# The last tile of a down product on row halves of the array, next to the attention scores, and new durations in a list schedule

## The chip, the cores and the metric

The kernel runs on one core of a Trainium2 chip. The core has five engines with a queue of instructions each: TensorE (PE in the profile, with its weight loads as PEld), VectorE (DVE), ScalarE (ACT), GpSimd (POOL) and SyncE (SP, which issues the DMAs). They wait for each other through semaphores. The metric is the time of one execution on the device in microseconds (us).

## The reference

Everything is float32. The input x is 2 batches of 4096 tokens with 256 channels. Two blocks follow each other, each added to its input.

```python
# first block: a recurrence over the tokens, 256 channels side by side
x = x + group_norm(sigmoid(r) * wkv(k, v)) @ W_o.T       # r, k, v: products of mixed tokens
# second block: DEPTH = 2 layers of this
h = shift_token(x)                        # half of the channels come from the token before
q, k, v = split(h @ wqkv)                 # 8 heads of 64
q, k = rotary_xpos(l2norm(q) * qs, l2norm(k) * ksc)
sim = q @ k.T ; attn = softmax(sim)       # blocks of 128 tokens, own block and the one before
x = x + (attn @ v) @ wo
h = layernorm(shift_token(x)) * lg + lb
a, g = split(h @ w1 + b1)                 # 682 columns each
x = x + (a * gelu(g)) @ w2 + b2
```

The hidden width is 682 = 5 x 128 + 42. Together with a row of ones, which carries the bias b2, the last line is a product over 683 rows: five tiles of 128 rows and one of 43.

## The kernel before, in words

**Tiling.** A window is 128 tokens, a block of tokens four windows (512 tokens). The two layers over two batches give 32 blocks and 128 windows, numbered n = 0 to 127. Window n has its attention at its own place in the program; the feed-forward part (the hidden product with `w1`, the gelu, the product with `w2`, called the down product) is done per block, one block later, in portions (`fill`) put between the attention parts of the windows that follow. The recurrence of batch 0 is done ahead of window 0; that of batch 1 is cut into 16 chunks of 256 tokens (`rec2`), and chunk c is put at window `int(c * R_SLOTS / rec2.n)`: windows 0, 3, 6, 10 and so on to 50.

**One window's attention.** Four score banks are written by eight pairs of matmuls over 64 rows (`scores`): the even head of a pair works on the rows 0 to 63 of the array and the odd head on the rows 64 to 127. In the same unbroken run of TensorE instructions (a `piece`) stands `values(n - 1)`, the product of the probabilities of the window before with its v, on column halves of the array. `softmax` then works on one score bank after the other: a masked copy, a minimum, two exponentials with their sums, a reciprocal, and two scalings (`scaled`). `transpose_p` first adds one column of the probabilities to the next (on VectorE, four heads at once), and transposes the probabilities on TensorE.

**The feed-forward part of block k.** `gate` makes five hidden tiles of 128 rows and copies them to `hm`; `remainders` makes the 42 rows that are left of both halves; `gelus` runs over the six tiles of `hm`; `value` multiplies the other half in; `down(k, w)` multiplies the six tiles of `hm` with `w2` for window w of the block, six matmuls of 128 rows by 256 columns into one bank, adds the bank to x, and sends x out. The sixth tile is filled up with rows that meet zeros of `w2`, and takes a matmul over 128 rows as the others do. In the profile each float32 matmul of the program stands as two instructions.

**What sets the order.** The program notes all operations with a row number (`plan.at`), and a list scheduler (`Plan.order`) then decides the order on every engine: it keeps a clock for each engine, takes the operation that can start first, and among those that can start within 1 ns of each other the one with the lowest row. It works with durations that are written down in `Plan.cost` and `TURN` (what it charges TensorE for a change between the full array, row halves and column halves), and with eight PSUM banks: a piece that opens several banks is placed only when so many are free. An operation noted on `either` goes to ScalarE or VectorE, to whichever can begin it first. The order that comes out is fixed in the program; on the chip each queue just follows it and waits where it must.

Nearly all instructions are issued by one line (L503), so the profile's groups are told apart by tiles: `bank<-w,hm` is the down product, `bank<-kT,qT` the scores, `bank<-pT,vt` and `bank<-pB,dv` the values, `bank<-wqkv,xT` the q, k and v products, `bank<-hT,w` the hidden products, `bank<-wo,oT` the attention's output product, `bank<-mats,...` transposes. L497 and L499 are the scalings on VectorE and ScalarE.

Of the kernel before, what the change touches and what calls it, by code (L numbers as in the profile page):

```python
# [15 lines left out]
P = 128  # L16
# [17 lines left out]
R_SLOTS = 54  # L34
# [24 lines left out]
TURN = {"row": 195, "col": 95, "full": 95}  # L59
# [114 lines left out]
class Plan:  # L174
# [119 lines left out]
    def cost(self, o):  # L294
# [19 lines left out]
        elif o.eng == "vector":  # L314
            if name == "tensor_tensor_reduce":
                d = 210 + 1.05 * n
            elif name == "tensor_tensor_scan":
                d, o.lock = 2.48 * n, True
            elif name in ("scalar_tensor_tensor", "tensor_tensor"):
                d, o.lock = 175 + 1.04 * n, wide > 1  # L320
            elif name in ("tensor_scalar", "tensor_copy") and not psum:
                d, o.lock = 230 + 0.45 * n, n > 64
            elif name == "bn_aggr":
                d = 180
            elif name == "reciprocal":
                d = 165 + 4 * n
            else:
                d = 150 + 1.04 * n
            o.step, o.time = max(d - 70, 60), d
        elif o.eng in ("scalar", "either"):  # L330
            d = 160 + 0.83 * n
            if name == "scaled":
                d = 40 + 1.4 * n
            if name == "activation":
                o.set = SETS.get(o.args[2])
                if "accum_out" in o.kw:
                    d += 320
                elif o.args[2] in (AF.Gelu, AF.Identity):
                    d = 40 + 1.4 * n
            o.step, o.time = d - 100, d  # L340
        elif o.eng == "gpsimd":
            if name == "tensor_tensor":
                d = 600 + 160 * n if ALU.pow in o.args else 150 + 2.25 * n
                o.lock = n > 64
            elif name == "tensor_scalar":
                d = 200 + 1.12 * n
                o.lock = n > 64
            else:
                d = 170 + 0.98 * n
                o.lock = n > 64  # L350
# [10 lines left out]
    def order(self):  # L361
# [47 lines left out]
        while todo:  # L409
# [23 lines left out]
            for o in g:  # L433
# [12 lines left out]
                if o.eng == "either" and e == "vector":  # L446
                    n = o.outs[0].idx.size
                    time = 150 + 1.04 * n if o.name == "copy" else 230 + 0.45 * n
                    step = time - 70
                    o.lock = o.name == "scaled"  # L450
# [56 lines left out]
def kernel(ctx: ExitStack, tc: tile.TileContext, a: dict, out: bass.AP):  # L507
# [322 lines left out]
    def weights(l, which):  # L830
# [6 lines left out]
        if "1" in which:  # L837
            nc.sync.dma_start(out=w1, in_=a["w_1"][l])
            nc.sync.dma_start(out=w2, in_=a["w_2"][l])
# [5 lines left out]
    hm = tile_of([P, NM, T], "hm")  # L845
# [6 lines left out]
    xs, xTs, hs, x1s, zs, hTs, rems = ({} for _ in range(7))  # L852
# [179 lines left out]
    def scores(n):  # L1032
# [8 lines left out]
        with piece():  # L1041
            if n:
                values(n - 1)
            for hp in range(HEADS // 2):
# [10 lines left out]
    def softmax(n, g):  # L1055
# [36 lines left out]
        nc.vector.reciprocal(sums, sums)  # L1092
        for m in range(2):
# [3 lines left out]
    def transpose_p(n, s):  # L1097

        pr = prs[n]
        if not lone(n):
            p0 = pr[:, 4 * s : 4 * s + 4, 1]
            nc.vector.tensor_tensor(p0, p0, pr[:, 4 * s : 4 * s + 4, 0], ALU.add)
# [110 lines left out]
    def remainders(k):  # L1215
        pm = hidden(k, G_LAST * P, HS)
        nc.scalar.copy(hm[:HR, NM - 1, :], pm[64:HS])
        rems[k] = tile_of([P, T], "rem")[:HR]
        either(rems[k], pm[:HR])

    def gelus(k):
        l = blocks[k][0]
        with piece():
            for m in range(NM):
                rows = P if m < NM - 1 else HR
                g = hm[:rows, m, :]
                nc.scalar.activation(g, g, AF.Gelu, bias=b1[:rows, l, 1, m : m + 1])

    def value(k, m):
        l = blocks[k][0]  # L1230
        rows = P if m < NM - 1 else HR
        src = hidden(k, G_LAST * P + HS + m * P, P) if m < NM - 1 else rems.pop(k)
        g = hm[:rows, m, :]
        plan.early = k == NK - 1
        nc.vector.scalar_tensor_tensor(
            g, src[:rows], b1[:rows, l, 0, m : m + 1], g, ALU.add, ALU.mult
        )
        plan.early = False

    def down(k, w):  # L1240
        py = bank([P, D])
        for m in range(NM):
            nc.tensor.matmul(
                py, hm[:, m, w * P : (w + 1) * P], w2[:, m, :], start=(m == 0), stop=(m == NM - 1)
# [8 lines left out]
    def fill(n, i):  # L1253

        s = n % NW
        if s == 0:
            k = n // NW - 2
            if k >= 0:
                if i < 3:
                    down(k, i + 1)  # L1260
            return
# [12 lines left out]
        elif i < 3:  # L1274
# [3 lines left out]
        else:  # L1278
            down(k, 0)
# [6 lines left out]
        for t, n in (("h", 2), ("hT", 1), ("sq", 1), ("t2", 1), ("qk", 2), ("x", 4))  # L1286
        for i in range(n)
    ]
    lent = [(p, 0) for p in lent] + [(plan.places["hm_0"], i * 2 * T) for i in range(NM // 2)]
# [52 lines left out]
    nc.gpsimd.memset(hm[:, NM - 1, :], 1.0)  # L1342
# [13 lines left out]
    for n in range(NN + 6):  # L1356
# [5 lines left out]
        for c in range(rec2.n):  # L1362
            if int(c * R_SLOTS / rec2.n) == n:
# [24 lines left out]
        elif n == NN:  # L1388
            with piece():
                values(n - 1)  # L1390
# [36 lines left out]
        if w == 0 and NW < n < NN and (n - NW) % (NB * NW) == 0:  # L1427
            weights(n // (NB * NW) % L, "12")
# [30 lines left out]
def _laid_out(i):  # L1459
# [19 lines left out]
    pad = NM * P - HID - 1  # L1479
    w2 = np.concatenate([n("L0_ffn_w2"), n("L0_ffn_b2")[:, None, :]], 1)  # L1480
    w2 = np.pad(w2, ((0, 0), (0, pad), (0, 0)))
    d["w_2"] = w2.reshape(L, NM, P, D).transpose(0, 2, 1, 3)
    b1 = np.pad(n("L0_ffn_b1").reshape(L, 2, HID), ((0, 0), (0, 0), (0, NM * P - HID)))
# [25 lines left out]
```

## Time and profile before

| what | value |
| --- | --- |
| median of 3 runs | 3045.44 us (3045.35 to 3046.44) |
| the profiled execution's own time | 3047.84 us |
| its span, first to last instruction | 3046.0 us |
| mean granted TensorE clock | 0.994 |
| busy: PE, DVE, ACT, POOL | 2977.8, 2513.2, 1731.2, 1434.7 us |

A group's row names the line, engine and operation, the tiles written and read, the partitions and elements of one instruction and the count; then the busy time of the group, the mean duration of one in ns, and the idle time of its engine just before it with what ended most of it. The duration of a matmul is longer than its distance to the next, since matmuls are pipelined; the distance is read from the starts in the timeline. "PE busy" therefore says that the array has work, and PE's idle time is what the other engines cost it.

### The profile page before, as it was taken

The numbers are of one execution on the slowest core, as the hardware profiler recorded it, in microseconds if no ns is written. First come the engines' busy times: TensorE is split into PE (matmuls) and PEld (weight loads), VectorE is DVE, ScalarE is ACT, GpSimd is POOL, SyncE is SP. The second block draws the span as 40 slices with busy tenths as digits, with TensorE's granted clock in tenths as the row PEclk, the third lists the DMA queues.
The fourth block names the chain that finished last, engine by engine and source line by source line (L and its number), as shares of the span: only waits on it lengthen the run. The fifth ranks groups of instructions, "written<-read, shape, count | busy, mean of one in ns | idle before, by whom it ended". The sixth has DMA issues, their size and how long they took to land.

```text
span 3046.0 us, 47917 instructions
## 1 busy us (share of the span) xinstructions
PE 2977.8 (98%) x15500; PEld 1932.6 (63%) x15500; DVE 2513.2 (83%) x5487; ACT 1731.2 (57%) x4592; POOL 1434.7 (47%) x1705
## 2 busy tenths in 40 slices
PE   8979999999999999999999999999999999999998
PEld 3456566666666666666666666666666666666665
DVE  7889999989889898887787787878878787877774
ACT  6877665666556666655555455545545555555542
POOL 2227555445444545444455444444444554554541
PEclk9989999999999999999999999999999999999999
DMA  3222112111112121111112211112112111111110
GB/s 96 88 76 89 44 57 63 53 58 51 59 51 80 54 69 54 53 53 56 53 54 82 83 58 60 57 59 60 54 45 66 61 59 56 55 53 51 48 43 23
DMA packets 178163, 181.66 MB, mean 60 GB/s; under 512 B 27028, under 2 KB 147700, under 8 KB 177400
## 3 DMA queue, kind: packets, MB, share of 16 engines
q1 hardware_dynamic: 177912, 178.59, 19.0%
q8 instruction: 123, 2.02, 0.3%
q14 instruction: 128, 1.05, 0.1%
HBM read 78.38 MB, written 33.55 MB: 37 GB/s over the span
## 4 chain that ended last, share of the span: by engine, by line
PE 75%; DVE 13%; ACT 6%; issue 2%; POOL 2%; SPq 1%; DMA 1%; DVEq 0%; POOLq 0%; ACTq 0%
PE bank L503 75%; DVE arena L503 3%; ACT arena L503 2%; DVE sq L503 1%; DVE qk L503 1%; ACT L503 1%; DVE bank L503 1%; SPq L503 1%; DVE nmx L503 1%; DVE x L503 1%; ACT pr L499 1%; DVE pr L497 1%; DMA h<-x 1%; DVE hm L503 1%; POOL rs L503 1%
## 5 line engine op out<-in xcount | busy, mean ns | idle before, releaser
L503 PE MATMUL bank<-wqkv,xT 128*128 128x512 f32 x1536 | 728.1, 598 | 0.0
L503 PE MATMUL bank<-hT,w 128*128 128x512 f32 (+1 forms) x1408 | 646.7, 595 | 0.2 <-DVE hT L503 0.2
L503 POOL TENSOR_TENSOR t<-qk,tab 128x256 f32<-128x256 f32 x512 | 379.8, 762 | 502.5 <-DVE qk L503 293.8
L503 ACT ACTIVATE pr<-bank,nmx 128x129 f32<-128x129 f32 (+1 forms) x1024 | 362.4, 365 | 332.3 <-DVE nmx L503 331.8
L503 PEld LDWEIGHTS bank<-hT,w 128*128 128x128 f32 (+1 forms) x1408 | 257.6, 190 | 273.1 <-issue 256.4
L503 PEld LDWEIGHTS bank<-wqkv,xT 128*128 128x128 f32 x1536 | 269.1, 190 | 240.1 <-issue 230.4
L503 POOL TENSOR_TENSOR rn<-rn,mhalf 128x16 f32<-128x16 f32 x128 | 386.1, 3017 | 10.3
L503 PE MATMUL bank<-w,hm 128*128 128x256 f32 x1536 | 351.8, 379 | 0.0
L503 PEld LDWEIGHTS bank<-w,hm 128*128 128x128 f32 x1536 | 287.1, 190 | 51.1 <-issue 15.3
L499 ACT ACTIVATE pr<-pr,sums 128x129 f32<-128x129 f32 (+1 forms) x738 | 260.0, 398 | 40.6 <-DVE sums L503 38.0
L503 PE MATMUL bank<-kT,qT 64*128 64x256 f32 (+1 forms) x2048 | 252.4, 386 | 0.0
L503 PE MATMUL bank<-wo,oT 128*128 128x256 f32 x1024 | 248.0, 385 | 2.5 <-ACT oT L503 1.7
L503 PEld LDWEIGHTS bank<-wo,oT 128*128 128x128 f32 x1024 | 189.7, 190 | 74.7 <-issue 35.4
L503 DVE TENSOR_TENSOR pB<-bank,backs 128x512 f32<-128x512 f32 x248 | 169.3, 683 | 51.8 <-ACT pT L503 50.0
L503 PEld LDWEIGHTS bank<-kT,qT 64*128 64x128 f32 x2048 | 185.3, 186 | 39.0 <-issue 15.9
L503 PEld LDWEIGHTS bank<-mats,pr 128*128 128x128 f32 (+1 forms) x1148 | 130.8, 135 | 120.2 <-issue 40.3
L503 DVE COPY_PREDICATED bank<-packs,bank 128x254 f32<-128x254 int32 x496 | 186.0, 420 | 25.1 <-PE bank L503 24.9
L503 ACT ACTIVATION_READ_ACCUMULATOR pr<-bank,nmx 128x1 f32 x1024 | 206.7, 202 | 0.0
L503 PE MATMUL bank<-pT,vt 128*64 128x128 f32 x2048 | 203.6, 279 | 0.0
L503 PE MATMUL bank<-mats,pr 128*128 128x128 f32 (+1 forms) x1148 | 173.3, 275 | 22.1 <-DVE pr L503 18.8
L503 PE MATMUL bank<-arena,wold 128*128 128x256 f32 (+1 forms) x600 | 193.7, 447 | 0.4 <-DMA wold<-in_w_rkv_dram 0.4
L503 POOL TENSOR_TENSOR tab<-tab,qks 128x256 f32<-128x256 f32 x128 | 109.6, 857 | 177.2 <-DMA tab<-in_c_rot_dram 167.3
(148 smaller groups left out, 5440.6 us busy)
## 6 DMA issues: line engine op xcount, KB each, us to landing
vr<-vt SPq DMA_DIRECT2D x124, 224.0 KB
tab<-in_c_rot_dram SPq DMA_DIRECT2D x128, 128.0 KB
kT<-kT SPq DMA_DIRECT2D x64, 256.0 KB
z<-zd SPq DMA_DIRECT2D x16, 512.0 KB
x<-in_x_dram SPq DMA_DIRECT2D x16, 512.0 KB
x1d<-x SPq DMA_DIRECT2D x16, 512.0 KB
x<-x1d SPq DMA_DIRECT2D x16, 512.0 KB
h<-x SPq DMA_DIRECT2D x128, 64.0 KB
```

The costliest lines, as they stand in the source:

```text
L497: self.nc.vector.tensor_scalar(dst, src, scale, None, ALU.mult)
L499: self.nc.scalar.activation(dst, src, AF.Copy, scale=scale)
L503: getattr(getattr(self.nc, o.eng), name)(*args, **kw)
```

## The change

- **The sixth tile of the down product.** It leaves `hm` (now five tiles) for a tile `ends` of 128 rows by two windows by 128 tokens: the 43 rows of the block's even windows lie on partitions 0 to 42, those of its odd windows on partitions 64 to 106. The 43 rows of `w2` (and of the biases `b1`) are laid out twice, on the same partitions. `down_ends` multiplies them for two windows at once, one on the rows 0 to 63 and one on the rows 64 to 127 of the array, into two banks. It stands in the piece of `values` and `scores`, between the two, in the first and the second window of each block. `down` takes over these two banks and adds the five full tiles. All four `down` now stand at the first filling place of these two windows, two in each, where they stood at the last place of the window before (one) and at three places of the first window (three).
- `remainders`, `gelus` and the last `value` work on `ends` in two halves of 256 columns, where they worked on 512.
- **The column that is added.** It moves from `transpose_p` (once for four heads, after the scalings) to `softmax` (once for two heads, between the reciprocal and the scalings).
- **The scheduler's durations** are replaced, mostly by longer ones: `scaled` on 129 columns by ScalarE goes from 221 to 403 ns, on VectorE from 288 to 281 ns; the change back to the full array from 95 to 199 ns.
- **The recurrence's chunks** of batch 1 start five windows later and lie closer: windows 5, 8, 11, 14 and so on to 51.
- `w2` is loaded one window later than `w1` (it is in use one window longer); `pB` joins the buffers that the recurrence of batch 0 borrows.

```diff
...
-R_SLOTS = 54
+R_SLOTS = 50
-TURN = {"row": 195, "col": 95, "full": 95}
+TURN = {"row": 195, "col": 95, "full": 199}
...
-        elif o.eng in ("scalar", "either"):
-            d = 160 + 0.83 * n
-            if name == "scaled":
-                d = 40 + 1.4 * n
-            if name == "activation":
-                o.set = SETS.get(o.args[2])
-                if "accum_out" in o.kw:
-                    d += 320
-                elif o.args[2] in (AF.Gelu, AF.Identity):
-                    d = 40 + 1.4 * n
-            o.step, o.time = d - 100, d
+        elif o.eng in ("scalar", "either"):
+            d = (160 if psum else 195) + 0.83 * n
+            if name == "scaled":
+                d = 305 + 0.76 * n
+            elif name == "activation":
+                o.set = SETS.get(o.args[2])
+                if o.args[2] == AF.Identity:
+                    d = 365 + 0.87 * n
+                elif isinstance(o.kw.get("bias"), View):
+                    d += 85
+            o.step, o.time = d - 100, d
+            if "accum_out" in o.kw:
+                o.time = d + 200
...
             nc.sync.dma_start(out=wo, in_=a["w_o"][l])
         if "1" in which:
             nc.sync.dma_start(out=w1, in_=a["w_1"][l])
+        if "2" in which:
             nc.sync.dma_start(out=w2, in_=a["w_2"][l])
     kT = tile_of([P, HEADS // 2, 3, W], "kT")
...
+    hm = tile_of([P, NM - 1, T], "hm")
+    ends = tile_of([P, NW // 2, P], "ends")
...
         with piece():
             if n:
                 values(n - 1)
+            down_ends(n)
             for hp in range(HEADS // 2):
                 for r in range(2):
                     s, m = divmod(hp, 2)
...
                 accum_out=sums[:, m : m + 1],
             )
         nc.vector.reciprocal(sums, sums)
+        if not lone(n):
+            p0 = prs[n][:, h0 : h0 + 3 : 2, :]
+            nc.vector.tensor_tensor(p0[:, :, 1], p0[:, :, 1], p0[:, :, 0], ALU.add)
         for m in range(2):
             ph = prs[n][:, h0 + 2 * m, off:]
             nc.either.scaled(ph, ph, sums[:, m : m + 1])
...
     def transpose_p(n, s):
         pr = prs[n]
-        if not lone(n):
-            p0 = pr[:, 4 * s : 4 * s + 4, 1]
-            nc.vector.tensor_tensor(p0, p0, pr[:, 4 * s : 4 * s + 4, 0], ALU.add)
         ppt = bank([P, 4, W])
         for h in range(4):
             nc.tensor.transpose(ppt[:, h, :], pr[:, 4 * s + h, 1:], ident)
...
     def remainders(k):
         pm = hidden(k, G_LAST * P, HS)
-        nc.scalar.copy(hm[:HR, NM - 1, :], pm[64:HS])
-        rems[k] = tile_of([P, T], "rem")[:HR]
-        either(rems[k], pm[:HR])
+        rems[k] = tile_of([P, NW // 2, P], "rem")
+        for odd in range(2):
+            rows = slice(64 * odd, 64 * odd + HR)
+            nc.scalar.copy(ends[rows], of_half(pm[64:HS], odd))
+            either(rems[k][rows], of_half(pm[:HR], odd))
+    def of_half(t, odd):
+        return t.rearrange("p (w two t) -> p w two t", two=2, t=P)[:, :, odd, :]
     def gelus(k):
         l = blocks[k][0]
         with piece():
-            for m in range(NM):
-                rows = P if m < NM - 1 else HR
-                g = hm[:rows, m, :]
-                nc.scalar.activation(g, g, AF.Gelu, bias=b1[:rows, l, 1, m : m + 1])
+            for m in range(NM - 1):
+                g = hm[:, m, :]
+                nc.scalar.activation(g, g, AF.Gelu, bias=b1[:, l, 1, m : m + 1])
+            for odd in range(2):
+                rows = slice(64 * odd, 64 * odd + HR)
+                g = ends[rows]
+                nc.scalar.activation(g, g, AF.Gelu, bias=b1[rows, l, 1, NM - 1 : NM])
     def value(k, m):
         l = blocks[k][0]
-        rows = P if m < NM - 1 else HR
-        src = hidden(k, G_LAST * P + HS + m * P, P) if m < NM - 1 else rems.pop(k)
-        g = hm[:rows, m, :]
         plan.early = k == NK - 1
-        nc.vector.scalar_tensor_tensor(
-            g, src[:rows], b1[:rows, l, 0, m : m + 1], g, ALU.add, ALU.mult
-        )
+        if m < NM - 1:
+            src = hidden(k, G_LAST * P + HS + m * P, P)
+            g = hm[:, m, :]
+            nc.vector.scalar_tensor_tensor(g, src, b1[:, l, 0, m : m + 1], g, ALU.add, ALU.mult)
+        else:
+            src = rems.pop(k)
+            for odd in range(2):
+                rows = slice(64 * odd, 64 * odd + HR)
+                g = ends[rows]
+                nc.vector.scalar_tensor_tensor(
+                    g, src[rows], b1[rows, l, 0, m : m + 1], g, ALU.add, ALU.mult
+                )
         plan.early = False
+    def down_ends(n):
+        k, i = (n - NW) // NW - 1, n % NW
+        if not 0 <= k < NK or i > 1:
+            return
+        for odd in range(2):
+            rows = slice(64 * odd, 64 * odd + 64)
+            pys[k, 2 * i + odd] = bank([P, D])
+            nc.tensor.matmul(
+                pys[k, 2 * i + odd], ends[rows, i, :], w2[rows, NM - 1, :], start=True, stop=False
+            )
     def down(k, w):
-        py = bank([P, D])
-        for m in range(NM):
+        py = pys.pop((k, w))
+        for m in range(NM - 1):
             nc.tensor.matmul(
-                py, hm[:, m, w * P : (w + 1) * P], w2[:, m, :], start=(m == 0), stop=(m == NM - 1)
+                py, hm[:, m, w * P : (w + 1) * P], w2[:, m, :], start=False, stop=(m == NM - 2)
             )
         x = xs[k][:, w, :]
         nc.vector.tensor_tensor(x, x, py, ALU.add)
...
     def fill(n, i):
         s = n % NW
-        if s == 0:
-            k = n // NW - 2
-            if k >= 0:
-                if i < 3:
-                    down(k, i + 1)
-            return
+        k = n // NW - 2
+        if s < 2 and 0 <= k < NK and i == 0:
+            down(k, 2 * s)
+            down(k, 2 * s + 1)
         k = n // NW - 1
         if not 0 <= k < NK:
             return
...
                 gelus(k)
             elif i < 3:
                 value(k, i - 1)
-        elif i < 3:
+        elif s == 3 and i < 3:
             value(k, i + 2)
             if i == 2:
                 value(k, 5)
-        else:
-            down(k, 0)
...
         if here:
             transpose_qk(n)
         for c in range(rec2.n):
-            if int(c * R_SLOTS / rec2.n) == n:
+            if NW + 1 + int(c * R_SLOTS / rec2.n) == n:
                 plan.at(n + 0.5)
                 if AHEAD <= c + 1 < rec2.n:
                     rec2.ahead(c + 1, rec2.mixed)
...
         if here:
             scores(n)
             differences(n)
-        elif n == NN:
+        else:
             with piece():
-                values(n - 1)
+                if n == NN:
+                    values(n - 1)
+                down_ends(n)
         if behind:
             kept(n - 1)
         if here:
...
         fill(n, 2)
         fill(n, 3)
-        if w == 0 and NW < n < NN and (n - NW) % (NB * NW) == 0:
-            weights(n // (NB * NW) % L, "12")
+        if w < 2 and NW < n < NN and (n - NW - w) % (NB * NW) == 0:
...
```

## The prediction

> **What bounds the kernel now.** I read the page first (busy time, slices, chain, groups), then the timeline of TensorE in one late window, the busy time by stretch of windows, and TensorE's waits.
>
> ```profile
> PE   8979999999999999999999999999999999999998
> DVE  7889999989889898887787787878878787877774
> ...
> PE 75%; DVE 13%; ACT 6%; issue 2%; POOL 2%; SPq 1%; DMA 1%; DVEq 0%; POOLq 0%; ACTq 0%
> ...
> L503 PE MATMUL bank<-w,hm 128*128 128x256 f32 x1536 | 351.8, 379 | 0.0
> ```
>
> TensorE is full in all but the first slices, and the chain lies on it for 75% of the span. The w,hm row is the down product: 768 matmuls in 1536 instructions.
>
> The timeline (start, length, group):
>
> ```profile
> 1508.48 2.75 PE L503 MATMUL bank<-w,hm 128*128 128x256 f32 x12
> 1511.07 1.04 PE L503 MATMUL bank<-mats,qk 128*128 128x128 f32 x8
> ...
> 1515.34 0.39 PE L503 MATMUL bank<-pB,dv 128*64 128x128 f32 x4
> 1515.65 2.00 PE L503 MATMUL bank<-kT,qT 64*128 64x256 f32 x16
> 1517.58 1.98 PE L503 MATMUL bank<-wqkv,xT 128*128 128x512 f32 x4
> ```
>
> One down product (12 instructions) takes 1511.07 - 1508.48 = 2.59 us, 0.216 each. The scores, 16 instructions of the same 256 columns on alternating row halves, take 1.93 us, 0.121 each with the changes of mode in it: two halves really run side by side.
>
> Busy time by stretch; the stretches are windows 0-4, 5-7, 20-35, 36-51 and 66-97:
>
> ```profile
> core 0: us, PE busy (x) PEld busy (x) DVE busy (x) ACT busy (x) POOL busy (x), PEclk, DMA share, GB/s
> 259.60:343.50 83.90, 76.03 (x455) 50.80 (x456) 77.16 (x186) 51.38 (x159) 57.73 (x67) 0.96 0.21 66
> 343.50:406.40 62.90, 61.34 (x329) 37.64 (x326) 59.90 (x140) 45.40 (x116) 35.87 (x44) 1.00 0.14 40
> ...
> 682.70:1060.60 377.90, 369.75 (x1959) 245.52 (x1957) 333.78 (x722) 229.48 (x593) 185.17 (x218) 0.99 0.19 59
> 1060.60:1414.20 353.60, 347.85 (x1890) 228.91 (x1886) 309.08 (x665) 216.79 (x576) 174.39 (x201) 1.00 0.18 55
> ...
> 1707.40:2382.40 675.00, 674.60 (x3663) 443.80 (x3661) 538.87 (x1212) 346.38 (x1004) 311.17 (x376) 1.00 0.20 59
> ```
>
> Once the second recurrence is done (windows 66-97) TensorE idles 0.4 us of 675: a us taken from it there is a us of time. Beside the recurrence it idles about 2%, with VectorE at 88%. TensorE's waits, longest row of the whole run:
>
> ```profile
> PE bank L503 <- DVE pr L503: 18.8, 27, 2.3
> ```
>
> This is the added column of the probabilities, which the transposes wait for; 11.8 us of it fall between 406 and 1400 us.
>
> **What the Trainium skill says.** "TensorEngine Tiling (Array Packing)", Key Properties: tiles of a mode run in parallel, and a change of mode drains the array. The trace agrees: 0.121 against 0.216 us, and the step from pB to kT is 0.31 us where four such instructions otherwise take 0.22, so about 0.1 us a change. Same page, Gotcha 1: row tiles write to different PSUM banks and so raise PSUM pressure; here each half gets a bank of its own, and no row of before prices that. "TensorE: Matmul & The Clock Gate", Architectural detail: VectorE's and ScalarE's queues are strictly in order, so one late operation holds a bank's copy behind it.
>
> **The change, part by part**, against the profiled execution (3047.84 us, span 3046.0; the median of the runs, 3045.44, is 0.6 below the span).
>
> *Sixth tile.* Removed: 128 windows x 2 instructions x 0.216 = 55.3 us. Added: as many instructions in pairs, 256 x 0.108 = 27.6 us if a pair costs one instruction of full rows, 256 x 0.121 = 31.0 at the scores' mean. The pair stands between the values (column halves) and the scores (row halves), so the changes of mode stay as many, except at windows 128, 129, 132 and 133, where no scores follow: seven more, 0.7 us. I take -27.6 + 0.7 = -26.9 (bounds -26.9 and -23.6), nearly all of it in time that TensorE fills.
>
> *The added column* now goes ahead of the scalings; the transposes wait for the scalings alone. At best the 18.8 us vanish, at worst the scalings (0.40 us on ScalarE) arrive as late: 0. I take -9.
>
> *VectorE's load.* The order of the built program counts: column additions 248 -> 496 (0.16 to 0.25 us each against 61.5 us in all: about +40 us); scalings on VectorE 286 -> 418, 132 x 0.31 (84.9/274) = +41; copies of 512 columns out of PSUM, net +36 x 0.68 = +24; `rem` copies 18 of 512 columns -> 51 of 256, 51 x 0.42 - 12.2 = +9; multiplications of the sixth tile 32 -> 64, 64 x 0.48 - 27.4 = +3. Together +117 us, 0.9 a window; ScalarE loses 132 x 0.40 = 53 us of scalings. Per window, windows 66-97: TensorE 21.1 -> 20.9, VectorE 16.8 -> 17.7, still cover. Windows 20-35 (five chunks before and after): TensorE 23.1 -> 22.9, VectorE 20.9 -> 21.8, 95% of it. A chunk costs (23.1 - 21.1) x 16/5 = 6.5 us of TensorE and (20.9 - 16.8) x 16/5 = 13 of VectorE; windows 36-51 get six instead of five: TensorE 21.7 - 0.2 + 0.4 = 21.9, VectorE 19.3 + 0.9 + 0.8 = 21.0, 96%. The nearest row to such a load is windows 5-7, VectorE at 95%, where TensorE idles 2.5% against 2.2% in windows 20-35. I take one more point of idle over 44 windows of 22 us: +10 (bounds 0 and +30).
>
> *Banks.* The piece opens seven of eight banks in 64 windows, where it opened five, and two stay open until `down` ends. In the built order the shortest TensorE work between two uses of a score bank falls from 5.4 to 3.2 us; twelve reuses are under 4.5 us, before none. Emptying the first score bank takes 0.42 + 0.42 + 2 x (0.36 + 0.20) = 2.0 us (masked copy, minimum, two exponentials with sums) and hand-overs, so it just fits. I take +2 (bounds 0 and twelve times 0.8, +10); the large version is a rival.
>
> *The chunks' places.* Windows 0-7 lose two of three chunks, 13 us of TensorE and 26 of VectorE; windows 8-51 get them. If the 9.4 us that TensorE idles in windows 0-7 stay, this is 0 (bounds -9, when VectorE's relief ends that idle, and +5).
>
> *At nothing:* four short ScalarE copies a block for two long ones, a seventh gelu (hidden by ScalarE's idle 43% of the span; uncovered 0.6 us x 32 = 19); the separate load of `w2`, which waits for the last `down` of the old layer, with tables and shifted rows behind it on SP, three windows (60 us) before its use (uncovered 3 loads x some us); other buffers and order in the recurrence of batch 0, 0 (bounds +-3).
>
> Sum: -26.9 - 9 + 10 + 2 = -24 on 3046.0, so 3022; the 0.6 us to the median are below its precision.
>
> **Rivals.**
> 1. *VectorE becomes the bound beside the recurrence.* For it: 95% of TensorE's time in windows 20-51. If TensorE idles 3 points more there (+30 instead of +10), 3042. Against it: at 95% before (windows 5-7) it idled only 2.5%.
> 2. *Slower: seven banks stall the piece.* Each of the 64 pieces waits for the bank of the product before it to be copied out behind other work in an in-order queue. The gain left is 24 us, so it decides from 24/64 = 0.38 us a piece; at 0.6 us, 3022 + 38 = 3060. For it: TensorE's reserve of free banks falls from three to one. Against it: in 117 of 128 windows a product of 1.72 us stands ahead of the piece, longer than the copy of the bank before it (0.58 to 0.68 us), and before no wait of TensorE for banks shows in windows 66-97.
> 3. *More than foreseen:* true durations and the moved addition end most idle time beside the recurrence: -26.9 - 19 and 0 for VectorE, 3000.
> 4. *It doesn't do what it says:* the halves run one after the other, 55.3 us again, about 3048. The scores' 0.121 us speaks against it.
>
> **How the numbers follow.** A measurement here tells about 0.2%, 6 us, from no change. Forecast 0.63 (its own range 3006 to 3036), rival 1 0.13, rival 2 0.09, rival 3 0.12, rival 4 0.03. Faster: forecast 0.62, rival 3 0.12, the lower part of rival 1 0.04: 0.78. Slower: rival 2 0.09 and the top of rival 1 0.02: 0.11. The rest, 0.11, within 0.2%. The range 3003 to 3043 leaves out rival 2, rival 4, and the outer ends of 1 and 3.
>
> **What would show it.** The w,hm group falls to 1280 instructions, and a group of 256 on 64 rows stands between values and scores at 0.11 to 0.12 us each. Windows 66-97 shorten from 675.0 to about 668 (32 x 0.216 = 6.9), with TensorE's idle still under 2 us. VectorE's busy time is near 2630 us. The wait for the added column falls below 10 us. I am wrong if TensorE shows idle time ahead of the values, the ends or the scores in windows 66-97 (banks), if its idle share in windows 20-51 goes beyond 4% (VectorE), or if the pair takes 0.2 us an instruction.

## The result and the profile after

The changed kernel takes 3072.99 us (3072.23 to 3074.23) against 3045.94 us of the kernel before in the same comparison: ratio 1.0083, 95% interval 1.0068 to 1.0098. It is 27 us slower, and the interval lies clear of 1; the forecast was 3022 us. The profiled execution took 3073.15 us, its span is 3071.1 us, its mean granted clock 0.991 (before 0.994).

The page of the kernel after, the rows that answer to those of before:

```profile
PE   9979999999999999999999999999999999999998
DVE  7989988989889989898888888888888888888884
...
PE 64%; DVE 22%; ACT 6%; issue 3%; POOL 3%; DMA 1%; SPq 1%; DVEq 0%; ACTq 0%; POOLq 0%
...
L506 PE MATMUL bank<-w,hm 128*128 128x256 f32 x1280 | 288.5, 380 | 0.0
```

The down product lost its 256 instructions, and TensorE still looks full in every slice. But the chain of work that ended last leaves TensorE more often: 64% instead of 75%, and VectorE holds 22% of it instead of 13%.

The pair itself, in TensorE's timeline of a window like the one shown of before (start, length, group):

```profile
2027.89 0.39 PE L506 MATMUL bank<-pB,dv 128*64 128x128 f32 x4
2028.21 0.70 PE L506 MATMUL bank<-w,ends 64*128 64x256 f32 x4
2028.74 1.89 PE L506 MATMUL bank<-kT,qT 64*128 64x256 f32 x16
2030.57 0.70 PE L506 MATMUL bank<-wqkv,xT 128*128 128x512 f32 x1
```

Four instructions of the pair take 2028.74 - 2028.21 = 0.53 us, a change of mode in it, where the old ones took 4 x 0.216 = 0.86; the scores behind them take 1.83 instead of 1.93 us. That fits their finding the array on row halves already: with the pair elsewhere (e16 below) they take 2015.46 - 2013.53 = 1.93 us again. The 0.31 us from pB to the pair are the same step as before. Nothing waits ahead of the pair or the scores. So this part does what the diff says.

Busy time by stretch (start:end, us, then busy time and instructions of PE, its weight loads, DVE, ACT, POOL, clock, DMA), windows 0-4, 5-7, 20-35, 36-51 and 66-97:

```profile
255.70:337.00 81.30, 74.95 (x451) 50.38 (x452) 76.31 (x188) 56.73 (x168) 58.75 (x68) 0.96 0.22 69
337.00:396.80 59.80, 57.37 (x312) 34.39 (x310) 57.35 (x139) 41.63 (x112) 31.00 (x41) 1.00 0.11 30
...
678.70:1055.30 376.60, 363.27 (x1937) 240.01 (x1937) 339.75 (x781) 224.90 (x585) 182.14 (x216) 0.99 0.19 59
1055.30:1427.10 371.80, 358.64 (x1934) 236.02 (x1932) 336.19 (x757) 218.76 (x579) 184.26 (x210) 1.00 0.18 55
...
1724.20:2409.10 684.90, 673.45 (x3668) 437.38 (x3665) 564.23 (x1325) 333.23 (x986) 319.89 (x378) 1.00 0.19 58
```

Subtract PE's busy time from each length. Beside the recurrence (windows 20-51) the idle time goes from 13.9 to 26.5 us. In windows 66-97, where it had been 0.4 us and where every us taken from TensorE was to be a us of time, it is 11.5 us, and the stretch grew from 675.0 to 684.9 us instead of shrinking to 668. VectorE is at 82% there: it is not full.

TensorE's waits (what for, us in total, times, longest), two rows of before and then those of the kernel after:

```profile
PE bank L503 <- DVE h L503: 5.6, 1, 5.6
PE bank L503 <- DVE qk L503: 4.6, 8, 1.4
...
PE bank L506 <- DVE qk L506: 31.1, 31, 2.9
PE bank L506 <- ACT pr L502: 15.3, 22, 3.4
...
PE bank L506 <- DVE h L506: 9.4, 3, 4.7
PE bank L506 <- ACT pr L506: 6.7, 6, 3.4
PE bank L506 <- DVE pr L500: 5.3, 11, 1.2
```

All three places are transposes: of the normed q and k (4.9 us of idle time ahead of them before, 31.1 now), of the probabilities (19.2 before, 22.4 now) and of h (5.6 before, 16.2 now). There TensorE takes up what a chain of small operations on VectorE, ScalarE and GpSimd has made. The three account for 40 us; over the whole span TensorE idles 102.6 us instead of 68.2.

A pause also costs more than its idle time. First, a transpose's modelled length (0.27 us) reaches over its distance to the next (0.11), so the beginning of a wait is booked as busy: the probabilities' transposes show 164.4 us of busy time instead of 156.5 (a part of this may be the clock). Second, the clock. TensorE's timeline in window 17 and the busy time of 3.4 us just after:

```profile
599.81 0.60 PE L506 MATMUL bank<-mats,h 128*128 128x128 f32 x4
603.79 1.11 PE L506 MATMUL bank<-mats,h 128*128 128x128 f32 x4 [3.37 <-ACT pr L506]
```

```profile
603.60:607.00 3.40, 3.21 (x10) 2.77 (x11) 3.40 (x15) 3.40 (x16) 1.61 (x1) 0.53 0.07 17
```

After 3.37 us without work the array runs at about half clock (0.53) for 3.4 us. The Trainium skill, "TensorE: Matmul & The Clock Gate", Part 1, What's actually happening, has this: the array is cold after about 3.4 us of idleness and at half rate until as long of work. The half rate and its 3.4 us are seen here; the 3.4 us of idleness are no limit in these traces. In the same kernel the clock is 0.50 for 3.4 us from 829.1 and from 1696.1 us, after pauses of only 1.86 and 2.36 us, and in e3 below it stays at 1.00 after a pause of 3.40 us that ends at 1767.91 us. The mean clock, 0.991 instead of 0.994, is by an estimate from these rounded values 3071 x 0.009 - 3046 x 0.006 = 9 us.

### The profile page after: what moved, and what is told of

Same layout as the page of the kernel before. It is cut to its first block, busy times and chain, and to the rows that moved or that the text cites. A ratio compares the mean times of both kernels' runs of the same rounds, so it can differ in the third digit from the quotient of the medians.

```text
span 3071.1 us, 48744 instructions
## 1 busy us (share of the span) xinstructions
PE 2968.5 (97%) x15500; PEld 1914.7 (62%) x15500; DVE 2609.7 (85%) x5969; ACT 1667.2 (54%) x4485; POOL 1424.4 (46%) x1705
## 4 chain that ended last, share of the span: by engine, by line
PE 64%; DVE 22%; ACT 6%; issue 3%; POOL 3%; DMA 1%; SPq 1%; DVEq 0%; ACTq 0%; POOLq 0%
PE bank L506 64%; DVE arena L506 4%; DVE qk L506 2%; ACT pr L506 2%; DVE sq L506 2%; DVE bank L506 2%; DVE rn L506 2%; DVE x L506 2%; DVE pr L500 1%; DVE nmx L506 1%; DVE pB L506 1%; POOL rn L506 1%; ACT L506 1%; ACT arena L506 1%; POOL rs L506 1%
## 5 line engine op out<-in xcount | busy, mean ns | idle before, releaser
L506 POOL TENSOR_TENSOR rn<-rn,mhalf 128x16 f32<-128x16 f32 x128 | 398.0, 3110 | 10.2
L506 PE MATMUL bank<-w,hm 128*128 128x256 f32 x1280 | 288.5, 380 | 0.0
L506 PEld LDWEIGHTS bank<-w,hm 128*128 128x128 f32 x1280 | 242.6, 191 | 33.4 <-issue 1.0
L502 ACT ACTIVATE pr<-pr,sums 128x129 f32<-128x129 f32 (+1 forms) x606 | 225.2, 414 | 52.1 <-DVE pr L506 48.3
L506 PEld LDWEIGHTS bank<-mats,pr 128*128 128x128 f32 x1148 | 133.6, 135 | 157.8 <-issue 63.3
L506 ACT ACTIVATION_READ_ACCUMULATOR pr<-bank,nmx 128x1 f32 x1024 | 217.1, 212 | 0.0
L506 PE MATMUL bank<-mats,pr 128*128 128x128 f32 x1148 | 178.0, 276 | 22.4 <-ACT pr L502 15.3
L506 ACT ACTIVATE sq<-qk 128x1024 f32<-128x1024 f32 x128 | 136.0, 1063 | 114.2 <-DVE qk L506 113.1
L506 PE MATMUL bank<-pB,dv 128*64 128x128 f32 x1984 | 194.2, 273 | 3.6 <-DMA pB<-last 2.8
```

Source lines behind the costliest of these rows:

```text
L502: self.nc.scalar.activation(dst, src, AF.Copy, scale=scale)
L506: getattr(getattr(self.nc, o.eng), name)(*args, **kw)
```

## The experiments

The ratios are to the kernel before, measured on the same chip; its median there was 3047.0, 3046.7 (e9 to e12), 3045.9 (e13 to e16) and 3045.8 us (e17, e18). The first question was which part of the change costs the time.

### The parts

**All old durations in the kernel after**, and **the new durations alone in the kernel before**:

```diff
 # e1_old_durations: after                    # e2_durations_alone: before
-                d = 240 + 1.04 * n           -                d = 210 + 1.05 * n
+                d = 210 + 1.05 * n           +                d = 240 + 1.04 * n
...
-TURN = {"row": 195, "col": 95, "full": 199}  -TURN = {"row": 195, "col": 95, "full": 95}
+TURN = {"row": 195, "col": 95, "full": 95}   +TURN = {"row": 195, "col": 95, "full": 199}
```

> The changed kernel with all of the scheduler's durations and TURN of before put back; the pair of row halves, the moved column addition and the chunks' places stay. Theory D (the new durations make an order in which the chain that ends in the transposes of q and k, and the scalings ahead of the transposes of the probabilities, arrive too late): 3020 to 3035 us, and TensorE's wait for qk back under 10 us. Theory B (the pair's banks: seven of eight in the piece, two held until down): 3060 us or more. Theory P (the column addition, twice as often and ahead of the scalings): 3060 us or more.

> The kernel before with only the new durations and TURN. Theory D: slower than before, 3060 to 3085 us, with TensorE waiting for qk some 25 us. Theories B and P: 3040 to 3050 us, since neither the pair nor the moved addition is in it.

Measured: 3049.71 us, ratio 1.0011 (1.0002 to 1.0020), and 3079.98 us, 1.0104 (1.0089 to 1.0120). The durations, which change no operation, cost 23 us in the kernel after and 33 us in the kernel before. They are most of the loss of 27.

**The pair alone**: the sixth tile on row halves with the new places of `down`, but old durations, old chunks, and the column added where it was. **The pair and the moved column**: the same with the addition moved.

```diff
 # e3_pair_alone: before
+            down_ends(n)
...
+        py = pys.pop((k, w))
+        for m in range(NM - 1):
...
 # e12_pair_and_addition: e3, and
         nc.vector.reciprocal(sums, sums)
...
+            nc.vector.tensor_tensor(p0[:, :, 1], p0[:, :, 1], p0[:, :, 0], ALU.add)
```

> The kernel before with only the sixth tile on row halves and the places of down that go with it (old durations, old column addition, old places of the chunks). Theory D: 3018 to 3032 us, the 27 us of TensorE nearly whole. Theory B: 3050 us or more. Theory P: as theory D.

> The pair alone (3038.6 us) with the column addition moved as the change does, old durations and old places of the chunks. Theory P (the addition twice as often loads VectorE, and the scalings wait for it): 3045 to 3052 us, most of the 11 us between the pair alone and the run with the old durations. If the chunks' places are what costs them: 3035 to 3042.

Measured: 3038.55 us, 0.9970 (0.9958 to 0.9982), and 3038.28 us, 0.9978 (0.9969 to 0.9987). The pair is a gain, of 8.5 us. The moved column is worth nothing beside it. From e12 to e1 only the chunks' places differ: 11 us slower, little above what a mere re-planning does (below), so it is not shown that the places themselves cost anything.

**The column back in `transpose_p`**, in the kernel after, is the same test from the other end:

```diff
-            nc.vector.tensor_tensor(p0[:, :, 1], p0[:, :, 1], p0[:, :, 0], ALU.add)
...
+            nc.vector.tensor_tensor(p0, p0, pr[:, 4 * s : 4 * s + 4, 0], ALU.add)
```

> The changed kernel with the column addition put back into the transposes of the probabilities (four heads at once, after the scalings). Theory P: 3040 to 3055 us, VectorE's busy time 20 to 40 us less. Theory D: within 10 us of the changed kernel's 3073 us, qk still waited for 20 us or more. Theory B: the same as theory D.

Measured: 3072.52 us, 1.0085 (1.0068 to 1.0102): 0.5 us from the kernel after. With the old addition TensorE idles 43.8 us ahead of the transposes of the probabilities (28.0 of them for the added column) and 12.6 ahead of those of q and k; with the moved one 22.4 and 31.1. What is gained at one place is waited for at the other.

**Half of the sixth tile left out** in the kernel before: in the odd windows of each block the down product has five tiles, and nothing takes the place of the sixth.

```diff
+        tiles = NM - w % 2
-        for m in range(NM):
+        for m in range(tiles):
```

> The kernel before with the sixth tile of the down product left out in the odd windows: 64 x 2 x 0.216 = 27.6 us of TensorE's work are gone and nothing is put in their place (the sums of these windows lack 43 rows, the bias among them). If TensorE's time is the kernel's time, as the prediction had it: 3018 to 3025 us, and the pair's remaining 19 us are a cost of the pair (banks, its small operations, a later down). If not, because work in front of TensorE sets the pace of the windows beside the recurrence: 3030 to 3042 us, as the pair alone.

Measured: 3030.27 us, 0.9941 (0.9926 to 0.9956). TensorE's busy time falls by 2977.8 - 2949.7 = 28.1 us, exactly as with the pair alone, and the time by 16.8 us: six tenths of it. In windows 66-97, 16 x 2 x 0.216 = 6.9 us are left out, the stretch shrinks by 3.7 (to 671.3 us), and TensorE's idle time grows from 0.4 to 3.1. Work taken from TensorE is not all time, even where it had no idle time at all: what it waits for is made no sooner. That is what half a sixth tile less brings here without any cost of its own; the pair brings half of that. (The 8 us between them are no more than what a re-planning moves.)

**The pair late**, in front of the two down products that it opens, so that its banks do not stand beside those of the scores:

```diff
 # e3, and
-            down_ends(n)
...
         if s < 2 and 0 <= k < NK and i == 0:
+            with piece():
+                down_ends(n)
             down(k, 2 * s)
```

> The pair alone (3038.6 us with its place between values and scores) with the pair moved to just ahead of the two down products that it opens: its two banks are then open only until these end, and do not stand beside the four of the scores. That costs two changes of mode for each of 64 pairs, about 64 x 0.2 = 13 us. If the banks are what the pair lost (8 us of the 16.8 us that leaving the tile out in half the windows brings), 3040 to 3045 us; if they cost nothing, 3048 to 3053 us.

Measured: 3057.04 us, 1.0029 (1.0015 to 1.0042): 18.5 us slower than in its place beside the scores, not faster. That lies above both expected ranges. In windows 66-97 the pair, the five tiles behind it and the scores, which must change the mode themselves again, take 5.0 us more from start to start (1.55, 1.75 and 1.66); four times that over the kernel is an estimate of 20 us, about the whole difference. So no gain from the banks is seen. But the 8 us that were looked for are as much as a re-planning moves, and a gain of that size could be hidden: this speaks against the banks and does not rule them out.

### How much is mere re-planning?

Each edit of a duration gives another order of the whole program, so three edits that mean nothing measure that: hand-overs between engines at 63 instead of 60 ns, VectorE's durations times 1.01, and the new price of a change back to the full array alone.

```diff
-SEM = 60           # e9_handover_63
+SEM = 63
...
+            d *= 1.01   # e10_vector_101
             o.step, o.time = max(d - 70, 60), d
...
-TURN = {"row": 195, "col": 95, "full": 95}   # e11_turn_199
+TURN = {"row": 195, "col": 95, "full": 199}
```

> The kernel before with the scheduler's hand-over time between engines at 63 ns instead of 60: no operation changes, only the order that comes out. Theory S (the order of before is a lucky one among many nearly equal ones, so that any re-planning costs about 10 us): 3052 to 3062 us. Theory D2 (the new durations are worse as durations): 3043 to 3051.

> The kernel before with all VectorE durations of the scheduler 1% longer; again only the order changes. Theory S: 3052 to 3062 us. Theory D2: 3043 to 3051.

> The kernel before with only the change back to the full array charged at 199 ns instead of 95 (the trace shows about 100). Theory S: 3052 to 3062 us, as any re-planning. Theory D2: 3047 to 3056, TensorE's work is planned 0.1 us a window too long and VectorE's and ScalarE's operations are promised too late for nothing.

Measured: 3051.02 us, 1.0019 (1.0012 to 1.0026); 3039.02 us, 0.9982 (0.9974 to 0.9991); 3046.95 us, 1.0001 (0.9993 to 1.0010). An order that differs by nothing that matters moves the time by up to 8 us in these three, and the order of the kernel before is no lucky one. The single parts of the change, 8 to 11 us each, are at the edge of this; the 23 and 33 us of the durations are beyond it.

### Which durations, and why

The new durations are not mostly longer where it counts. Those on the chains in front of the transposes became shorter: an exponential with its sum holds ScalarE for 252 ns in the plan instead of 487, the power over 16 columns takes GpSimd 2926 instead of 3160, and VectorE's plain products of two tensors take 25 ns less and free the engine 40 ns sooner.

**Those of one engine alone**, put into the kernel before:

```diff
 # e6_scalar_durations
-            d = 160 + 0.83 * n
+            d = (160 if psum else 195) + 0.83 * n
...
 # e7_gpsimd_durations
-                d = 600 + 160 * n if ALU.pow in o.args else 150 + 2.25 * n
+                d = 430 + 156 * n if ALU.pow in o.args else 140 + 2.22 * n
...
 # e13_vector_durations
-            o.step, o.time = max(d - 70, 60), d
+            o.step, o.time = max(d - 85, 60), d
```

> The kernel before with the new ScalarE durations only (VectorE's, GpSimd's and TURN as before). D1: carries most of the 33 us that all new durations cost: 3065 to 3080 us. D2: a third of it or less, 3050 to 3060.

> The kernel before with the new GpSimd durations only (the power on 16 columns goes from 3160 to 2926 ns). D1: 3043 to 3052 us, no difference. D2: a third of the 33 us, 3053 to 3062. A third theory, D3 (the power's margin of 0.2 us is what mattered, since the transposes of q and k wait behind it): 3065 or more.

> Kernel before with the new VectorE durations alone (the step of VectorE's operations and of `either` pieces on it included; ScalarE's and GpSimd's stay old). Two theories of the 33 us that all new durations cost together. Theory L: the loss is load, the new durations make VectorE look cheaper (its step is 15 ns shorter, its scalings 0.29 instead of 0.37 us), the list gives it more of the pieces that either engine can do, and TensorE waits for it. Then VectorE's busy time rises from 2513 to about 2600 us with these durations alone, and the time is 3060 to 3070 us. Theory M: the loss is margin, every engine's durations are now close to the true ones or under them and the plan packs without slack; then each engine's part costs about the same, 8 to 14 us, and this kernel takes 3052 to 3060 us whatever its VectorE load.

Measured: 3057.83 us, 1.0035 (1.0024 to 1.0045); 3055.57 us, 1.0025 (1.0017 to 1.0032); 3058.88 us, 1.0041 (1.0026 to 1.0055). The excesses, 0.35, 0.25 and 0.41%, add to 1.01%, against 1.04% of all together. Each is at or a little above what a re-planning moves, so the adding up is a hint and no proof; but no engine's table alone carries the loss. VectorE's busy time in the third is 2553 us, not the 2600 that the theory of load wants. (The scalings' duration on VectorE, which that expectation has at 0.29 instead of 0.37 us, goes from 288 to 281 ns by the formulas.)

**One duration that the trace contradicts.** ScalarE's timeline of the kernel after, the exponentials of a window:

```profile
2011.88 0.37 ACT L506 ACTIVATE pr<-bank,nmx 128x129 f32<-128x129 f32 x1
2012.15 0.19 ACT L506 ACTIVATION_READ_ACCUMULATOR pr<-bank,nmx 128x1 f32 x1
2012.24 0.36 ACT L506 ACTIVATE pr<-bank,nmx 128x129 f32<-128x129 f32 x1
...
2012.59 0.37 ACT L506 ACTIVATE pr<-bank,nmx 128x129 f32<-128x129 f32 x1
```

Each exponential with its sum is two instructions, and the next starts 0.35 us after it. The new durations let ScalarE go on after 160 + 0.83 x 129 + 85 - 100 = 252 ns; the old ones after 160 + 0.83 x 129 + 320 - 100 = 487. Eight of them in a window put ScalarE 8 x 0.1 = 0.8 us behind its plan. The edit, in the kernel after:

```diff
-                o.time = d + 200
+                o.step, o.time = d, d + 200
```

> The changed kernel with one duration altered: the scheduler holds ScalarE for 352 ns per exponential with a sum instead of 252 (the trace shows 0.35 us from one to the next; the durations of before held it for 487). Theory D1 (the loss by the durations comes from this one, which promises the probabilities 0.8 us too early in every window): 3045 to 3058 us, and TensorE's waits for the scalings and for qk halved. Theory D2 (the loss comes from the durations as a whole, which leave no margin): within 8 us of 3073.

Measured: 3063.24 us, 1.0053 (1.0036 to 1.0070): 10 us back, a little more than re-planning alone can do.

**Load or margin.** Two edits to the kernel after. One charges 150 ns for each hand-over instead of 60. That is no truer: in the chain shown further down VectorE ends at 2042.20 + 1.75 = 2043.95 and TensorE begins at 2044.01. It is slack, 90 ns for each link of a chain. The other leaves durations alone and gives an `either` piece to VectorE only if it can start there 300 ns sooner than on ScalarE.

```diff
-SEM = 60            # e14_margin
+SEM = 150
...
 # e15_prefer_scalar
-            e = min((e for e in engines if pick[e]), key=lambda e: pick[e][0], default=None)
+            wait = lambda e: 300 if e == "vector" and pick[e][1][0].eng == "either" else 0
+            e = min((e for e in engines if pick[e]), key=lambda e: pick[e][0] + wait(e), default=None)
```

> Kernel after with the planner's cost of every hand-over between engines raised from 60 to 150 ns: margin on each wait, durations as they are. Theory M (the plan lacks margin): the order leaves more time before each wait, and some 10 to 25 us come back, 3048 to 3063 us. Theory L (load on VectorE): 3065 us or more, since VectorE keeps its pieces. Orders that differ by nothing that matters moved the time by +4 and -8 us, so a difference under 8 us says nothing.

> Kernel after in which the planner gives a piece that either engine can do to VectorE only if it can start there over 300 ns earlier than on ScalarE; durations as they are. VectorE loses about 600 instructions (some 180 us of busy time), ScalarE gains them. Theory L: 3040 to 3055 us. Theory M: within 8 us of 3073 us, or slower, since ScalarE's exponentials then come later.

Measured: 3036.19 us, 0.9970 (0.9960 to 0.9980), and 3041.41 us, 0.9985 (0.9979 to 0.9992). Margin gives back 37 us. The busy time of both, e14 and then e15:

```profile
PE 2957.3 (97%) x15500; PEld 1911.9 (63%) x15500; DVE 2617.4 (86%) x6033; ACT 1645.4 (54%) x4422; POOL 1446.3 (48%) x1705
...
PE 2960.6 (97%) x15500; PEld 1911.5 (63%) x15500; DVE 2273.1 (75%) x5298; ACT 1961.6 (64%) x5157; POOL 1422.5 (47%) x1705
```

With margin VectorE does more than in the kernel after (2609.7 us), and the loss is gone all the same; so VectorE's load by itself is not the cause, and the theory of load, which wanted 3065 us or more, falls. But the theory of margin, taken alone, falls too: it wanted no gain from relieving VectorE, and that gives back 32 us (VectorE 2273.1 us). The reading that fits both: an order in which an operation is planned to arrive just in time, or sooner than it can, loses by being late; it can be mended by planning a later use, or by leaving the engine free enough to catch up. One rival stands untested: a plan with the durations as measured and still 60 ns a hand-over would tell how much of the loss is missing slack and how much is durations that are too short.

How it looks: TensorE's timeline from the scores of a window to the transposes of their probabilities, in the kernel after,

```profile
2007.34 2.00 PE L506 MATMUL bank<-kT,qT 64*128 64x256 f32 x16
...
2012.82 1.88 PE L506 MATMUL bank<-wqkv,xT 128*128 128x512 f32 x4
2014.54 0.27 PE L506 MATMUL bank<-mats,pr 128*128 128x128 f32 x1
2015.37 0.62 PE L506 MATMUL bank<-mats,pr 128*128 128x128 f32 x3 [0.56 <-ACT pr L502]
2015.82 1.88 PE L506 MATMUL bank<-hT,w 128*128 128x512 f32 x4
2017.54 1.08 PE L506 MATMUL bank<-mats,pr 128*128 128x128 f32 x5
```

and in the kernel after with margin:

```profile
1985.41 2.00 PE L506 MATMUL bank<-kT,qT 64*128 64x256 f32 x16
...
1992.60 1.88 PE L506 MATMUL bank<-hT,w 128*128 128x512 f32 x4
1994.32 1.15 PE L506 MATMUL bank<-mats,pr 128*128 128x128 f32 x9
1995.30 1.88 PE L506 MATMUL bank<-hT,w 128*128 128x512 f32 x4
```

Without margin the transposes stand 7.2 us after the scores. One can go; the others wait 0.56 us for a scaling, and the five behind the next product take 0.91 us to the next group (2018.45) instead of 0.54. With margin one more product stands ahead, the transposes come 8.9 us after the scores, and all nine go through in 0.98 us. Nothing was made faster; TensorE has other work until the chain is through. In windows 66-97 TensorE then idles 4.4 us instead of 11.5, and over the span 78.9 instead of 102.6.

The other long wait, for q and k, is a chain with one link that no fixed duration can hold. GpSimd, VectorE and TensorE in one stretch of the kernel after:

```profile
2037.95 4.21 POOL L506 TENSOR_TENSOR rn<-rn,mhalf 128x16 f32<-128x16 f32 x1
...
2042.20 1.75 DVE L506 TENSOR_TENSOR qk<-sq,rn 128x1024 f32<-128x1024 f32 x1 [0.56 <-POOL rn L506]
...
2044.01 1.09 PE L506 MATMUL bank<-mats,qk 128*128 128x128 f32 x8 [0.99 <-DVE qk L506]
```

The power takes 4.21 us here. The new duration is 430 + 156 x 16 = 2926 ns, which is what it takes at other places (2.94 us at 2010.34). Over all of them it is too short:

```profile
L506 POOL TENSOR_TENSOR rn<-rn,mhalf 128x16 f32<-128x16 f32 x128 | 398.0, 3110 | 10.2
```

The mean is 3110 ns, above the new duration and just under the old one, 600 + 160 x 16 = 3160; 48 of the 128 take longer than even that. (The scheduler keeps VectorE's products of two operands apart from GpSimd's operations over more than 64 columns, with `lock`; the power has 16 and is not kept apart.) In the same way VectorE's multiplication behind it is planned at 150 + 1.04 x 1024 = 1215 ns, 1240 before, and takes 1284 in the mean.

### Margin for both, and both cures

The control: the kernel before, with hand-overs at 150 ns. And the kernel after with both edits.

```diff
-SEM = 60            # e17_margin_on_before; e18_margin_and_scalar has it with the edit of e15
+SEM = 150
```

> Control for the margin: the kernel before, all its old durations, with the hand-over at 150 instead of 60 ns and nothing else. If the margin is a thing that only the new durations lack (the old ones carry it in over-long VectorE and accumulation times), it stays within 8 us of 3046 us, and the whole change, with margin 3036 us, is worth about 10 us like the pair alone. If any plan of this kernel gains from it, 3020 to 3037 us here, and then the comparison at equal margin says what the change itself is worth: nothing, or a loss.

> Kernel after with both edits that helped it: hand-over 150 ns (alone 3036 us) and VectorE only where it starts 300 ns earlier (alone 3041 us). If the two cure the same waits, 3030 to 3040 us; if they add, as far as the 27 us of work that TensorE lost allow, 3010 to 3025 us, and this is the fastest of all.

Measured: 3035.26 us, 0.9962 (0.9947 to 0.9977), and 3025.22 us, 0.9927 (0.9910 to 0.9943). The kernel before gains 10.5 us from margin where the kernel after gains 37: the difference of 26 us is, up to 1 us, the loss of the change. At equal margin the two stand at 3035.3 and 3036.2 us, and the change as a whole is worth nothing that can be told. With both edits the changed kernel is the fastest of all, 20.5 us below the kernel before: the two cures add only in part (37 and 32 us alone, 48 together). The kernel before with both edits was not run, so the 20.5 us are the edits' and not shown to be the change's.

## Why the prediction was wrong

By its own steps, with what the runs showed in place of each:

- **Sixth tile, -26.9 us: the step that failed in size.** The relief of TensorE was right (28.1 us of busy time with the pair alone), and so was the rate of a pair (0.53 us for four instructions with a change of mode in it, 0.1 of which the scores behind them save: 0.108 us an instruction, as reckoned). "Nearly all of it in time that TensorE fills" was wrong: leaving as much out brings 16.8 us, the pair 8.5. I read windows 66-97, where TensorE idled 0.4 us, as if a shorter TensorE would stay full. That stretch was full, but its supplies were hardly ahead of their uses: with half the tile left out it gave 3.7 us of 6.9 and began to wait. Where the 8 us between e3 and e8 go is not settled: e3 idles 15.9 us in windows 36-51 where before it was 5.8, about what a re-planning can do.
- **The added column, -9 us: wrong, 0** (e4, e12). The chain to the transposes is as long as it was. It was argued from the last name in a wait; with that name gone, TensorE waits as long in all for others, 53.5 us for probabilities and q and k together, against 56.4 with the old addition (e4).
- **VectorE's load, +10 us: the mechanism was wrong, and here the forecast was lost.** The load itself came nearly as reckoned (2609.7 us against 2630). But the new durations were priced only by the load that they shift. That they take the reserve out of chains in the plan, and in part fall below what the trace shows, was in no term and no rival; it is the +23 us between e1 and the kernel after. ScalarE's new formula stood in the diff and was not held against the starts in the trace, where the exponentials' 0.35 us against 252 ns stood to be read.
- **Banks, +2 us:** nothing seen. TensorE idles 0.0 us ahead of the pair and the scores; ahead of the values it idles 3.6 us, 2.8 of them for a DMA of `pB`, in the whole span and none of it in windows 66-97. (The emptying of a score bank was reckoned with 0.56 us for each exponential and its sum, end to end; they overlap, and the next starts after 0.35. The term was too careful, not too small.)
- **The chunks' places, 0:** 11 us slower between e12 and e1, within the bound only if re-planning is counted.

From run to run: -8.5 for the pair, 0 for the column, +11 for the chunks, +23 for the durations, together +26 on a measured +27. These are steps of one row of kernels and add up by construction; each carries the 8 us of a re-planning.

Of the rivals, the first (VectorE becomes the bound beside the recurrence) names the engine that waits are booked on, and is still not it: TensorE's idle share in windows 20-51 is 3.5%, under the 4% that was set, VectorE is at 90% there and not 96, and the run with more VectorE work is 37 us faster. The second, slower by banks, had the right side with a mechanism of which nothing is seen. What happened stood in none.

## What to carry to other kernels

A list schedule whose durations are the usual ones, or a little under them, has no slack: what arrives late is passed on along the fixed order, and the engine meant to be full waits. Measure durations from start to start in the trace, the helper instructions too, and then add margin on purpose, here 90 ns a hand-over; compare two kernels at equal margin, and take out first what an edit without meaning does to the time. And a us taken from the full engine is worth a us only if what it uses next is ready a us sooner.

## What the runs showed of the hardware

- An exponential over 129 columns with its sum takes ScalarE 0.35 us from start to start, as two instructions of 0.37 and 0.20 us that overlap.
- The power over 128 x 16 takes GpSimd 2.94 us in one place and 4.21 in another. In the kernel after, 37 of the 49 powers with VectorE's whole 1024-column product `sq<-sq,t` in their time take over 3.1 us, and seven, with both multiplications by `tab` in it too, 4.11 to 4.81; of the 65 without any of that product 55 take under 2.96. The multiplications by `tab` alone do not do it: in the kernel before, no power with both of them and none of that product takes over 2.95. The other way, VectorE's 1024-column multiplication `qk<-sq,rn` takes 1.75 us beside GpSimd's next operation, and at most 1.23 in the 69 places with no GpSimd work beside it. The Trainium skill, "GPSIMD Engine Reference", Specifications, says that the two share their SBUF interfaces and contend when VectorE reads two SBUF inputs. The first product fits that and the multiplications by `tab` alone do not; no run here took the overlap away, so the link is seen side by side and not shown as a cause.
